# Token-major copies of layer 1 made by VectorE block transposition and DMAs through DRAM instead of TensorE transposes

## The chip, the cores and the metric

The kernel runs on one core of a Trainium2 chip. The metric is device time in microseconds (us) from the start to the end of one execution. Three executions of the kernel before gave 2556.81, 2556.70 and 2556.46 us, a median of 2556.7 us.

## The reference, cut to what matters

Two layers over x of shape (4, 128, 64, 64): 4 batches, 128 channels, 4096 positions ("tokens"). Layer 0 is full self-attention over positions behind a group normalization. Layer 1 is causal self-attention and a recurrent feed-forward part, each behind a layer normalization over the 128 channels of a token:

```python
x = x + conv_attention(groupnorm(x))            # layer 0, full attention, queries and keys of 64 channels
t = to_tokens(x)                                # (b, 4096, 128)
t = t + causal_attention(ln_t(t), Wq, Wk, Wv)   # layer 1
t = t + ffn(ln_t(t), W, V, gamma, beta)         # batch norm over all tokens, then
#   y[t] = sigmoid(Wx[t] + y[t-1] @ V.T) along the tokens
def ln_t(v): return (v - mean(v, -1)) / sqrt(var(v, -1) + 1e-5)
```

The kernel holds x channel-major: channels on the 128 partitions, tokens along the free dimension. The layer normalization of a token reduces over channels, so it needs those values token-major: tokens on partitions, channels along the free dimension.

## The kernel before, in words

All arithmetic is fp32 (layer 0's keys and queries are split into two fp32r parts). The code that runs is `fast_kernel`. `general_kernel` is a fallback in a branch that is not taken here.

**Units.** Attention is cut into units. One unit is a pair of 128-row key blocks against one query tile of 512 columns. Layer 0 has 16 units for each of its 8 query tiles, layer 1 has 2(c+1) units for query tile c because it is causal. The order is batch by batch, layer 0 then layer 1, tile by tile: 128 + 72 units for a batch. `score(i)` puts the scores of unit i into a PSUM pair (L923 and L930, two buffers), ScalarE writes their exponentials to a tile `s` in SBUF (L932 and L936, three buffers), and `product(i - 1)` adds the exponentials to `total` on VectorE (L960, L965) and multiplies them by the values on TensorE (L968).

**Tasks between the units.** All other work is written as Python generators, and each `yield` ends a piece. Between `score(i)` and `product(i - 1)` the function `step()` takes one piece of each task in `ends` (the closing of a query tile, `finish`) and one piece of the first task in `todo`. `whole(key)` runs a task to its end at once. It is called where a unit needs the result. The tasks that matter here:

- `prepare1(b, c)` (key `p1`) is put on the list when query tile c of layer 0 is closed. It makes the normalized token-major values V1 and the reciprocal deviations R1 for 512 tokens.
- `ffn(b, c, ...)` (key `f`) is put on the list when query tile c of layer 1 is closed. It stores the tile to DRAM (`kept`, L751, batches 0 to 2), computes the reciprocal deviations of 512 tokens, and multiplies by the FFN weight.
- `after(b, c)` comes before `query1(b, c)`. It calls `whole` on every `p1` up to c.
- `keys0(b + 1, c)`, eight tasks, prepare the keys of the next batch's layer 0.

Both `prepare1` and `ffn` call `deviations` (L693): four TensorE transposes of 128x128 into a PSUM tile `pt` (L698), then on VectorE `bn_stats` (L702) and `bn_aggr` (L704) for each block and an addition (L570), then a power on GpSimd (L571). `prepare1` writes V1 from `pt` with four `tensor_scalar` (L731). `ffn` needs only the reciprocal deviations, which `spread` (L709) brings back channel-major.

**Buffers and queues.** `misc` tiles (PSUM, two buffers) hold `pt` and other small matmul results. `finish` calls `project`, which lets a stated number of pieces pass and then issues the matmul `po` (L831) and the residual addition (L834). SyncE issues the DMAs of X, of `kept` and of the reload at the end (L508, L751, L1015). After the attention the recurrence runs in chunks (L1045 to L1155). The order on an engine is not always the written order: the build may place an instruction that is ready ahead of one that waits.

Of the kernel before, what the change touches and what calls it, by code (L numbers as in the profile page):

```python
# [25 lines left out]
F32 = mybir.dt.float32  # L26
AF = mybir.ActivationFunctionType
ALU = mybir.AluOpType
# [446 lines left out]
def fast_kernel(  # L475
# [97 lines left out]
    with ExitStack() as actx:  # L573
# [10 lines left out]
        def misc(name):  # L584
            return ps_m.tile([P, QT], F32, tag="m", name=name)
# [104 lines left out]
            Q[b, 0, c] = q  # L690
            yield

        def deviations(src, eps, name):  # L693

            n = src.shape[-1] // P
            pt = misc(f"pt_{name}")
            for j in range(n):
                nc.tensor.transpose(pt[:, ts(j, P)], src[:, ts(j, P)], ident)  # L698
            stats = small.tile([P, 4, 6], F32, tag="lst", name=f"lst_{name}")
            mv = small.tile([P, 4, 2], F32, tag="lmv", name=f"lmv_{name}")  # L700
            for j in range(n):
                nc.vector.bn_stats(stats[:, j, :], pt[:, ts(j, P)])  # L702
            for j in range(n):
                nc.vector.bn_aggr(mv[:, j, :], stats[:, j, :])  # L704
            rstd = small.tile([P, 4], F32, tag="rstd", name=f"rstd_{name}")
            rsqrt(rstd[:, :n], mv[:, :n, 1], eps, n)
            return pt, mv, rstd[:, :n]

        def spread(r, name):  # L709

            n = r.shape[-1]
            g = small.tile([P, 4, 4], F32, tag="g", name=f"g_{name}")
            for q in range(4):
                nc.vector.tensor_copy(g[0:32, :n, q], r[ds(32 * q, 32), :])
            for q in range(1, 4):
                nc.vector.tensor_copy(g[ds(32 * q, 32), :n, :], g[0:32, :n, :])
            rb = tmp.tile([P, QT], F32, tag="r", name=f"rb_{name}", bufs=2)[:, : n * P]
            nc.vector.transpose(
                rb.rearrange("p (k j) -> p k j", j=32),
                g[:, :n, :].rearrange("p j q -> p (j q)").unsqueeze(2).to_broadcast([P, 4 * n, 32]),  # L720
            )
            return rb

        def prepare1(b, c):
            if c == 0:
                V1[b] = kv.tile([P, NB, C], F32, tag="V1", name=f"V1_{b}")
                R1[b] = small.tile([P, NB], F32, tag="R1", name=f"R1_{b}")
            pt, mv, rstd = deviations(X[b][:, ts(c, QT)], 1e-5, f"1_{b}_{c}")
            nc.gpsimd.tensor_copy(R1[b][:, ts(c, 4)], rstd)
            for j in range(4):  # L730
                nc.vector.tensor_scalar(  # L731
                    V1[b][:, 4 * c + j, :], pt[:, ts(j, P)], mv[:, j, 0:1], rstd[:, j : j + 1],
                    ALU.subtract, ALU.mult,
                )
            yield

# [9 lines left out]
        def ffn(b, c, off, w):  # L746
            name = f"f_{b}_{c}_{off}"
            cols = ds(c * QT + off, w)
            src = X2[b][:, cols]
            if b < len(kept):  # L750
                nc.sync.dma_start(out=kept[b][:, cols], in_=src)  # L751
            yield
            _, _, rstd = deviations(src, 1e-5, name)
            yield
            pw = misc(f"pw_{name}")[:, :w]
            if off == 0:
                wt[b, c] = tmp.tile([P, QT], F32, tag="w", name=f"w_{name}")
            part = wt[b, c][:, ds(off, w)]
            if w == QT - LAST:
                nc.tensor.matmul(pw, lhsT=FWc, rhs=src, start=True, stop=True)  # L760
                raw = tmp.tile([P, QT], F32, tag="a", name=f"raw_{name}")[:, :w]
                nc.scalar.copy(raw, pw)
                prow = misc(f"prow_{name}")
                idle(prow, 7)
                nc.tensor.matmul(prow[:, :w], lhsT=rstd.to_broadcast([P, P]), rhs=ident, start=True, stop=True)
                nc.vector.tensor_tensor(part, raw, prow[:, :w], ALU.mult)
                idle(misc(f"idle_{name}"), 5)
            else:
                rb = spread(rstd, name)
                nc.tensor.matmul(pw, lhsT=FWc, rhs=src, start=True, stop=True)  # L770
                nc.vector.tensor_tensor(part, pw, rb, ALU.mult)
            if w < QT:
                yield
            nc.scalar.copy(
                WX[b][:, :, ds((c * QT + off) // CHUNK[b], w // CHUNK[b]), :].rearrange("p l s t -> p s l t"),
                part.rearrange("p (s l t) -> p s l t", l=CHUNK[b] // 2, t=2),
            )
            if off + w == QT:
                nc.vector.bn_stats(stats_f[:, b * NQ + c, :], wt.pop((b, c)))
            yield  # L780

        def finish(b, layer, c, off, w, av, total):

            name = f"{layer}_{b}_{c}_{off}"
            k = w // 32
            if w == QT - LAST:

                pz = misc(f"pz_{name}")
                for h in range(2):
                    nc.tensor.matmul(pz[:, :w], lhsT=ones, rhs=total[:, h, :w], start=h == 0, stop=h == 1)  # L790
                idle(misc(f"idle_{name}"), 4)
                rb = tmp.tile([P, QT], F32, tag="a", name=f"rb_{name}")[:, :w]
                nc.vector.reciprocal(rb, pz[:, :w])
                o = tmp.tile([P, QT], F32, tag="b", name=f"o_{name}")[:, :w]
                nc.vector.scalar_tensor_tensor(o, rb, GUARD, av[:, :w], ALU.mult, ALU.mult)
                yield from project(b, layer, c, off, w, o, 0)
                return
            t = tmp.tile([P, QT], F32, tag="a", name=f"t_{name}")[:, :w]
            nc.vector.tensor_tensor(t, total[:, 0, :w], total[:, 1, :w], ALU.add)  # L799
            tt = tmp.tile([P, QT], F32, tag="b", name=f"tt_{name}")[:, :w]  # L800
            nc.vector.transpose(tt, t)  # L801
            part = small.tile([P, 16], F32, tag="part", name=f"part_{name}")
            nc.vector.tensor_reduce(part[:, :k], tt.rearrange("p (k j) -> p k j", j=32), AX.X, ALU.add)
            yield
            side = small.tile([32, 4, 16], F32, tag="side", name=f"side_{name}")
            for q in range(4):
                nc.vector.tensor_copy(side[:, q, :k], part[ds(32 * q, 32), :k])
            z = small.tile([P, 16], F32, tag="z", name=f"z_{name}")
            nc.vector.tensor_reduce(z[0:32, :k], side[:, :, :k].rearrange("j q k -> j k q"), AX.X, ALU.add)
            nc.vector.reciprocal(z[0:32, :k], z[0:32, :k])  # L810
            for q in range(1, 4):
                nc.vector.tensor_copy(z[ds(32 * q, 32), :k], z[0:32, :k])
            rb = tmp.tile([P, 16, 32], F32, tag="a", name=f"rb_{name}")[:, :k, :]
            nc.vector.transpose(rb, z[:, :k].unsqueeze(2).to_broadcast([P, k, 32]))  # L814
            o = tmp.tile([P, QT], F32, tag="b", name=f"o_{name}")[:, :w]
            nc.vector.scalar_tensor_tensor(  # L816
                o, rb.rearrange("p k j -> p (k j)"), GUARD, av[:, :w], ALU.mult, ALU.mult
            )
            yield from project(b, layer, c, off, w, o, 2 if w == QT else 5)

        def project(b, layer, c, off, w, o, waits):
            cols = ds(c * QT + off, w)
            xt = X[b][:, cols]
            if layer == 0:
                nc.vector.scalar_tensor_tensor(xt, o, 1.0 / GUARD, xt, ALU.mult, ALU.add)
                yield
                return
            for _ in range(waits):
                yield
            po = misc(f"po_{b}_{c}_{off}")[:, :w]  # L830
            nc.tensor.matmul(po, lhsT=W1v, rhs=o, start=True, stop=True)  # L831
            if c == 0:
                X2[b] = xpool.tile([P, N], F32, tag="X2", name=f"X2_{b}")
            nc.vector.scalar_tensor_tensor(X2[b][:, cols], po, 1.0 / GUARD, xt, ALU.mult, ALU.add)  # L834
            yield
# [4 lines left out]
        for b in range(B):  # L840
            for layer in range(2):
                for c in range(NQ):
                    parts = [(0, LAST), (LAST, QT - LAST)] if (b, layer, c) == (B - 1, 1, NQ - 1) else [(0, QT)]
                    for off, w in parts:
                        n = (c * QT + off + w) // P if layer else NB
                        units += [(b, layer, c, off, w, u, n) for u in range((n + 1) // 2)]
        todo, ends, made = [], [], {}

        def put(key, g):
            made[key] = g  # L850
# [132 lines left out]

        def step():

            for key in list(ends) + todo[:1]:
                if (key in ends or key in todo) and next(made[key], "done") == "done":
                    done(key)

        for _ in gn_stats(0):  # L990
            pass
# [204 lines left out]
```

## Time and profile before

| what | value |
|---|---|
| median of three runs | 2556.7 us |
| profiled execution | 2556.64 us |
| its span, first to last instruction | 2554.8 us |
| VectorE busy | 1771.1 us (69%), 3534 instructions |
| ScalarE busy | 1139.8 us (45%) |
| GpSimd busy | 194.7 us (8%) |
| DMA, mean over the span | 12 GB/s |
| mean granted TensorE clock | 0.997 |

The profile is of one execution. "Busy" is the time in which at least one instruction of an engine runs. Matmuls are pipelined, so TensorE's busy time says little about what one instruction costs. For that the reader wants the distance between the starts of neighbours, or the chain of work that ended last, which gives each piece the time for which it held up the end.

### The profile page before, as it was taken

Reading aid. Unit: us, or ns where it says so; the run is one execution under the profiler, and the core shown is the slowest. Engines: PE = TensorE matmul, PEld = TensorE weight load, DVE = VectorE, ACT = ScalarE, POOL = GpSimd, SP = SyncE. Lnnn points to the kernel's source line nnn. Section 1 sums busy time; section 2 is a strip of 40 time slices with the busy share of each in tenths; the row PEclk is TensorE's granted clock in tenths of the full one; section 3 lists DMA queues with packets and bytes.
Section 4 is the critical chain, followed back from the end, with each engine's and each line's share of the span. In section 5 each row is a group of like instructions: output and inputs, shape, how many; then the busy total and the mean of one; then the engine's idle time right before and its main releaser. Section 6 shows DMA issues by size and latency. Waiting matters only on the chain.

```text
span 2554.8 us, 22329 instructions
## 1 busy us (share of the span) xinstructions
PE 2506.5 (98%) x7612; PEld 1367.5 (54%) x7612; DVE 1771.1 (69%) x3534; ACT 1139.8 (45%) x1432; POOL 194.7 (8%) x281
## 2 busy tenths in 40 slices
PE   7999999999999999999999999999999999999997
PEld 4555554444555555444455555444455555544465
DVE  6776667656867667656777676855677675786567
ACT  4444444444444444444444444444444444444456
POOL 2010001101000100110000010011010000010000
PEclk9999999999999999999999999999999999999999
DMA  2000000000100000000100000000010000000013
GB/s 73 1 0 1 0 1 13 9 5 4 38 0 1 1 0 5 13 4 5 33 9 0 1 0 1 9 9 8 5 38 0 1 1 1 1 1 0 0 66 133
DMA packets 11946, 31.33 MB, mean 12 GB/s; under 512 B 2096, under 2 KB 2864, under 8 KB 10032
## 3 DMA queue, kind: packets, MB, share of 16 engines
q1 hardware_dynamic: 9216, 26.22, 2.8%
q10 hardware_dynamic: 2608, 3.61, 0.4%
q8 instruction: 61, 1.00, 0.2%
q14 instruction: 61, 0.50, 0.1%
HBM read 15.14 MB, written 14.68 MB: 12 GB/s over the span
## 4 chain that ended last, share of the span: by engine, by line
PE 88%; DVE 7%; ACT 2%; issue 1%; POOL 1%; POOLq 0%; DVEq 0%; ACTq 0%
PE av L968 48%; PE ps L930 17%; PE ps L923 16%; DVE total L965 2%; PE pv L675 1%; PE po L831 1%; PE pk L659 1%; PE pq L740 1%; PE pw_f L770 1%; PE pt L698 1%; ACT WX L1061 1%; ACT s L932 0%; POOL rstd_f L571 0%; PE pt_f L698 0%; PE pz L1060 0%
## 5 line engine op out<-in xcount | busy, mean ns | idle before, releaser
L965 DVE TENSOR_TENSOR total<-total,s 128x1024 f32<-128x1024 f32 (+5 forms) x810 | 882.1, 1092 | 561.0 <-ACT s L932 323.0
L968 PE MATMUL av<-s,WXp 128*128 128x512 f32 x2048 | 963.9, 593 | 1.7 <-ACT s L932 1.7
L932 ACT ACTIVATE s<-ps,shift 128x1024 f32<-128x1024 f32 x512 | 569.6, 1114 | 751.7 <-PE ps L930 728.3
L930 PE MATMUL ps<-q,K 128*128 128x512 f32 x2048 | 758.5, 492 | 1.0 <-DVE K L670 0.9
L936 ACT ACTIVATE s<-ps,zero,R 128x512 f32<-128x512 f32 (+3 forms) x607 | 405.1, 718 | 462.0 <-PE ps L923 460.5
L968 PEld LDWEIGHTS av<-s,WXp 128*128 128x128 f32 x2048 | 381.9, 189 | 299.1 <-issue 256.1
L930 PEld LDWEIGHTS ps<-q,K 128*128 128x128 f32 x2048 | 386.3, 189 | 289.7 <-issue 235.2
L968 PE MATMUL av<-s,V 128*128 128x512 f32 (+3 forms) x1214 | 505.0, 538 | 2.0 <-ACT s L936 1.7
L923 PE MATMUL ps<-q,X 128*128 128x512 f32 (+3 forms) x1214 | 503.5, 537 | 0.0
L923 PEld LDWEIGHTS ps<-q,X 128*128 128x128 f32 x1214 | 224.9, 190 | 236.3 <-issue 219.5
L968 PEld LDWEIGHTS av<-s,V 128*128 128x128 f32 x1214 | 222.0, 190 | 224.5 <-issue 195.6
L571 POOL TENSOR_TENSOR rstd<-rstd,mhalf 128x4 f32<-128x4 f32 x32 | 32.7, 1022 | 964.3 <-DVE rstd L570 964.3
L656 POOL TENSOR_SCALAR X<-X,B0v 128x512 f32<-128x512 f32 x32 | 67.6, 2114 | 250.9 <-DVE xg L654 249.4
L939 POOL TENSOR_SCALAR_AFFINE_SELECT s<-s 128x128 f32<-128x128 f32 x128 | 46.3, 366 | 519.5 <-ACT s L936 519.1
L731 DVE TENSOR_SCALAR V<-pt,lmv,rstd 128x128 f32<-128x128 f32 x128 | 43.7, 404 | 35.7 <-POOL rstd L571 35.7
L571 POOL TENSOR_TENSOR rstd_f<-rstd_f,mhalf 128x4 f32<-128x4 f32 (+2 forms) x33 | 35.8, 1086 | 406.3 <-DVE rstd_f L570 406.3
L689 DVE TENSOR_TENSOR q<-QR,qh 64x512 fp32r<-64x512 f32 x64 | 43.8, 685 | 6.3 <-PE ps L930 5.7
L671 ACT CAST K<-kh 64x512 fp32r<-64x512 f32 x32 | 19.7, 617 | 62.1 <-DVE kh L669 62.1
L799 DVE TENSOR_TENSOR t<-total 128x512 f32<-128x512 f32 x64 | 44.1, 689 | 4.4 <-PE pfw L615 2.5
L801 DVE STREAM_TRANSPOSE tt<-t 128x512 f32<-128x512 f32 x64 | 45.3, 708 | 1.9
L816 DVE SCALAR_TENSOR_TENSOR o<-rb,av 128x512 f32<-128x512 f32 x64 | 43.6, 682 | 4.1
L814 DVE STREAM_TRANSPOSE rb<-z 128x512 f32<-128x512 f32 x64 | 45.0, 703 | 1.1
(156 smaller groups left out, 1311.2 us busy)
## 6 DMA issues: line engine op xcount, KB each, us to landing
X<-in_x SPq DMA_DIRECT2D x28, 256.0 KB, 5.3
kept<-X SPq DMA_DIRECT2D x24, 256.0 KB, 2.0
Y<-kept SPq DMA_DIRECT2D x6, 1024.0 KB, 7.7
out<-Y SPq DMA_DIRECT2D x5, 1024.0 KB, 6.0
X<-in_x ACTq DMA_DIRECT2D x4, 256.0 KB, 5.5
out<-Y ACTq DMA_DIRECT2D x1, 1024.0 KB, 6.7
out<-X SPq DMA_DIRECT2D x1, 1024.0 KB, 10.9
out<-X ACTq DMA_DIRECT2D x1, 1024.0 KB, 13.3
```

The lines of the kernel that those rows point to most:

```text
L571: nc.gpsimd.tensor_tensor(dst, dst, mhalf[:, :n], ALU.pow)
L656: nc.gpsimd.tensor_scalar(xt, xt, B0v, None, ALU.add)
L799: nc.vector.tensor_tensor(t, total[:, 0, :w], total[:, 1, :w], ALU.add)
L801: nc.vector.transpose(tt, t)
L814: nc.vector.transpose(rb, z[:, :k].unsqueeze(2).to_broadcast([P, k, 32]))
L923: nc.tensor.matmul(ps[:, h, first[h] : w], lhsT=lhsT, rhs=q[:, off + first[h] : off + w], start=True, stop=True,)
L930: nc.tensor.matmul(ps[:, h, :], lhsT=lhsT, rhs=q[:, k, :], start=k == 0, stop=k == 1)
L932: nc.scalar.activation(s, ps, AF.Exp, bias=shift)
L936: nc.scalar.activation(part, ps[:, h, first[h] : w], AF.Exp, scale=scale, bias=zero)
L939: nc.gpsimd.affine_select(out=edge, in_=edge, pattern=[[1, P]], base=0, channel_multiplier=-1, compare_op=ALU.is_ge, fill=0.0,)
L965: nc.vector.tensor_tensor(t, t, s[:, h, f:w], ALU.add)
L968: nc.tensor.matmul(av[:, first[h] : w], lhsT=V[:, 2 * u + h, :], rhs=s[:, h, first[h] : w], start=u == 0 and h == 0, stop=2 * u + h == n - 1,)
```

## The change

`deviations` no longer transposes. It takes a token-major view `tok`. A new generator `turn` makes that view: VectorE transposes each 32x32 block of 128x512 (`nc.vector.transpose`), one DMA writes the result to a DRAM tile, and four DMAs, one for each group of 32 partitions, read it back in runs of 32 elements (128 bytes), so that each partition holds one token's channels in each of its four blocks. The destination is V1 itself in `prepare1`, which then normalizes it in place, and the turned tile in `ffn`. `turn` then yields 5. `step()` now skips a task for a stated number of units and takes the first task that does not wait. At most two turns are open at once. A third waits by yielding 1 up to eight times, then runs the oldest to its end. The last tile of the last batch keeps the TensorE transposes. The tile `r` goes from two buffers to one, `t` with two buffers is new, and `project` waits three pieces instead of two for the last tile of a batch.

```diff
-        def deviations(src, eps, name):
-
-            n = src.shape[-1] // P
-            pt = misc(f"pt_{name}")
-            for j in range(n):
-                nc.tensor.transpose(pt[:, ts(j, P)], src[:, ts(j, P)], ident)
+        def deviations(tok, n, eps, name):
+
...
-                nc.vector.bn_stats(stats[:, j, :], pt[:, ts(j, P)])
+                nc.vector.bn_stats(stats[:, j, :], tok[:, j, :])
...
+        turning = []
+
+        def turn(src, dst, name, key):
+
+            for _ in range(8):
+                if len(turning) == 2:
+                    yield 1
+            while len(turning) == 2:
+                whole(turning[0])
+            turning.append(key)
+            t = tmp.tile([P, QT], F32, tag="t", name=f"t_{name}", bufs=2)
+            nc.vector.transpose(t, src)
+            d = dram.tile([P, QT], F32, tag="turn", name=f"turn_{name}", bufs=4)
+            nc.sync.dma_start(out=d, in_=t)
+            if dst is None:
+                dst = t.rearrange("p (j c) -> p j c", c=C)
+            view = d.rearrange("(i r) (j q s) -> q r j i s", i=4, q=4, s=32)
+            for q in range(4):
+                nc.sync.dma_start(
+                    out=dst[ds(32 * q, 32)].rearrange("r j (i s) -> r j i s", i=4), in_=view[q]
+                )
+            yield 5
+            turning.remove(key)
+            return dst
...
-            rb = tmp.tile([P, QT], F32, tag="r", name=f"rb_{name}", bufs=2)[:, : n * P]
+            rb = tmp.tile([P, QT], F32, tag="r", name=f"rb_{name}")[:, : n * P]
...
-            pt, mv, rstd = deviations(X[b][:, ts(c, QT)], 1e-5, f"1_{b}_{c}")
+            tok = V1[b][:, 4 * c : 4 * c + 4, :]
+            yield from turn(X[b][:, ts(c, QT)], tok, f"1_{b}_{c}", ("p1", b, c))
+            mv, rstd = deviations(tok, 4, 1e-5, f"1_{b}_{c}")
             nc.gpsimd.tensor_copy(R1[b][:, ts(c, 4)], rstd)
             for j in range(4):
                 nc.vector.tensor_scalar(
-                    V1[b][:, 4 * c + j, :], pt[:, ts(j, P)], mv[:, j, 0:1], rstd[:, j : j + 1],
-                    ALU.subtract, ALU.mult,
+                    tok[:, j, :], tok[:, j, :], mv[:, j, 0:1], rstd[:, j : j + 1], ALU.subtract, ALU.mult,
                 )
...
-            _, _, rstd = deviations(src, 1e-5, name)
+            if (b, c) == (B - 1, NQ - 1):
+                pt = misc(f"pt_{name}")
+                for j in range(w // P):
+                    nc.tensor.transpose(pt[:, ts(j, P)], src[:, ts(j, P)], ident)
+                tok = pt.rearrange("p (j c) -> p j c", c=C)
+            else:
+                tok = yield from turn(src, None, name, ("f", b, c, off))
+            _, rstd = deviations(tok, w // P, 1e-5, name)
...
-            yield from project(b, layer, c, off, w, o, 2 if w == QT else 5)
+            yield from project(b, layer, c, off, w, o, 5 if w < QT else 3 if c == NQ - 1 else 2)
...
+            ready = [key for key in todo if pause.get(key, 0) <= 0][:1]
+            for key in pause:
+                pause[key] -= 1
+            for key in list(ends) + ready:
+                if key in ends or key in todo:
+                    got = next(made[key], "done")
+                    if got == "done":
+                        done(key)
+                    elif got:
+                        pause[key] = got
```

More of the change, by code (lines that the diff above doesn't have):

```diff
@@ L706, in deviations @@
             rsqrt(rstd[:, :n], mv[:, :n, 1], eps, n)
-            return pt, mv, rstd[:, :n]
+            return mv, rstd[:, :n]
+        turning = []
[20 more added lines that the diff above has]
+            return dst
         def spread(r, name):
@@ L846, in fast_kernel @@
                         units += [(b, layer, c, off, w, u, n) for u in range((n + 1) // 2)]
-        todo, ends, made = [], [], {}
+        todo, ends, made, pause = [], [], {}, {}
         def put(key, g):
@@ L984, in step @@
         def step():
-            for key in list(ends) + todo[:1]:
-                if (key in ends or key in todo) and next(made[key], "done") == "done":
-                    done(key)
+            ready = [key for key in todo if pause.get(key, 0) <= 0][:1]
[8 more added lines that the diff above has]
+                        pause[key] = got
         for _ in gn_stats(0):
```

## Prediction

> **What bounds the kernel now.** I read the busy shares first, then the chain of work that ended last in small windows, because a busy share doesn't price an instruction here.
>
> ```profile
> PE 2506.5 (98%) x7612; PEld 1367.5 (54%) x7612; DVE 1771.1 (69%) x3534; ACT 1139.8 (45%) x1432; POOL 194.7 (8%) x281
> PE 88%; DVE 7%; ACT 2%; issue 1%; POOL 1%; POOLq 0%; DVEq 0%; ACTq 0%
> ```
>
> TensorE is busy 98% of the span and holds 88% of the chain. VectorE has 31% to spare on the average. The chain in layer 0 of batch 0 (start us, us on the chain, what) gives the price of the four transposes:
>
> ```profile
> 303.00 0.70 PE ps L930 x3
> 303.70 0.43 PE pt L698 x4
> 304.13 1.72 PE av L968 x4
> 305.86 0.93 PE ps L930 x4
> 306.78 1.72 PE av L968 x4
> ```
>
> TensorE never stops here. A unit of layer 0 is 0.93 + 1.72 = 2.65 us, and one group of four transposes adds 0.43 us (0.44 in layer 1's windows). The by-form groups show why the busy column would mislead:
>
> ```profile
> L698 PE MATMUL pt_f<-ident,X 128*128 128x128 f32 x128 | 19.4, 273 | 0.4 <-DVE X L834 0.4
> L698 PE MATMUL pt<-ident,X 128*128 128x128 f32 x128 | 19.4, 274 | 0.8 <-DVE X L825 0.8
> ```
>
> 273 ns is the latency of one, and 19.4 us for 32 groups is 0.61 us each because it counts the last one's drain, which lies under the next matmul. The true slot is 0.435 us.
>
> VectorE matters where layer 1 ends and the next batch begins. The windows (us, then busy of PE, PEld, DVE, ACT, POOL, granted clock, DMA share, GB/s):
>
> ```profile
> 635.00:655.00 20.00, 17.79 (x63) 10.62 (x62) 16.86 (x53) 9.50 (x12) 3.19 (x5) 1.00 0.00 1
> 655.00:675.00 20.00, 20.00 (x59) 10.85 (x58) 18.39 (x44) 6.37 (x7) 2.01 (x2) 0.91 0.35 118
> 715.00:735.00 20.00, 20.00 (x62) 11.40 (x61) 10.79 (x10) 9.26 (x10) 0.00 (x0) 1.00 0.00 1
> ```
>
> VectorE is at 84 to 92% there against 54% in a quiet stretch, TensorE loses 2.2 us, and the clock drops right after. The timeline names the wait:
>
> ```profile
> 653.16 0.66 DVE L816 SCALAR_TENSOR_TENSOR o<-rb,av 128x512 f32<-128x512 f32 x1
> 653.88 1.12 PE L831 MATMUL po<-o,W1v 128*128 128x512 f32 x2 [2.21 <-DVE o L816]
> ```
>
> The closing of a batch's last tile is late on VectorE, and TensorE, in order, stands before `po`. The same stands at 1267 and 1880 us: three times some 2.4 us.
>
> **What the Trainium skill says.** "TensorE: Matmul & The Clock Gate", Part 4, puts a transpose at about 275 ns in one kernel's context. The trace agrees on the latency (273 ns), but the slot is 435 / 4 = 109 ns, and that decides. "VectorE: DVE Perf Modes", The three transpose paths: VectorE transposes only separate 32x32 blocks, so the blocks must still be moved between partitions, here by DMA. The trace has the instruction at this size (L801, 708 ns). "DMA: Bandwidth & Descriptors", Two DMAs through the same engine are not ordered: a read of what an earlier DMA wrote needs a wait on its semaphore at the issuing engine. No run here shows such a pair yet. I take it that SyncE stands between the write and the four reads.
>
> **The change, part by part**, against the profiled execution of 2556.64 us (span 2554.8), which is the median of 2556.7 for this purpose.
>
> *Transposes.* 32 tiles of `prepare1` and 31 of `ffn` (the last tile keeps its own): 63 groups x 0.435 = **-27.4 us** on the path. `pt` leaves the `misc` buffers too; no wait on it shows, so nothing is taken for that.
>
> *VectorE.* 63 block transposes x 0.71 = +44.7 us. `bn_stats` costs the same from SBUF (281 ns for 128 columns from PSUM; 682 ns for 512 from SBUF, L622: both are columns / 0.96 plus 148). V1's `tensor_scalar` now reads SBUF: L654 (SBUF, 512 columns) takes 562 ns, L664 (PSUM) 740. I put 128 columns at 360 ns against 404, so -6 us for 128; the bounds are 160 and 404. VectorE goes from 1771 to about 1810 us, 71%. In layers' middles this lies beside TensorE and costs 0. At the three batch boundaries, where VectorE is short, six FFN tiles fall into layer 0's small units: 6 x 0.71 = 4.3 us of new work each, 12.8 us in all. The cover is there for most, since the pauses also spread the tiles (two in twelve units, before one in four). I charge a third: **+4.2 us** (0 to 12.8).
>
> *The round trip.* SyncE issues 5 DMAs for each turn. A store of 256 KB lands in 2.0 us and a load of 256 KB in 5.3 us behind others:
>
> ```profile
> X<-in_x SPq DMA_DIRECT2D x28, 256.0 KB, 5.3
> kept<-X SPq DMA_DIRECT2D x24, 256.0 KB, 2.0
> ```
>
> Four reads of 64 KB, 0.33 to 0.5 us to issue each, in 2048 packets of 128 bytes. The trace's packets take 18 ns at 256 bytes and 27 at 512, so I estimate 13.5 ns at 128: 128 for each of 16 engines, 1.7 us. Write 2.0 + issue 0.3 + reads 3.3 to 6.5: **5.6 to 9 us**, doubled at worst if short packets write badly. The pause: `yield 5` is set after that step's count, and counted down before the list is read, so the task returns six steps later: 6 x 2.65 = 15.9 us in layer 0, 6 x 3.44 = 20.6 in layer 1. Hidden, cost 0. Without that cover, VectorE stands at `bn_stats`, and all `total` additions are queued behind it.
>
> *The forced turns.* Walking the task list by hand: `p1(b, 7)` for b = 0, 1, 2 comes behind eight `keys0` tasks, and `after(b, 7)`, at the head when tile 6 begins (unit 42 of layer 1), calls `whole` on it. The pause is passed over, so write, reads and `bn_stats` fall in one step. Three times VectorE may stand 5.6 to 9 us. Behind it are the `total` additions; those free the three `s` buffers, so exponentials and then TensorE wait. Around that place (531 to 548 us) the exponential at 547.9 us needs a `total` that ended at 544.7: 3.2 us of slack. But instructions written later already run ahead there (the closing's four steps, 530.3 to 533.1, precede the `bn_stats` at 533.07), which fills some 2.8 us. 5.6 + 0.7 - 3.2 - 2.8 is about nothing; 9 + 0.7 - 3.2 is 6.5, and a lowered clock adds 1.7 (at 655.5 to 658 matmuls took 0.85 instead of 0.43 us). I take 2 each: **+6.0 us** (0 to 24.6).
>
> *SyncE's queue.* 63 x (5 issues of 0.4 + a stand of 2.0) = 252 us of 2555. Queued behind are `kept` (wanted at the end), the reload of Y (likewise) and X of the next batch. X's eight loads (656.7 to 669 us, at full DMA rate) meet FFN turns twice and delay them by up to 10 us: 9 + 10 against a pause of 15.9. I charge 1 us each: **+2.0 us** (0 to 6). GpSimd's power and copies keep their counts, ScalarE's too.
>
> *`po` waits one unit more* for a batch's last tile: 2.65 us more for VectorE, where 3 x 2.4 us stand now, but VectorE has more to do. I take half: **-3.5 us** (0 to -9, with the clock drop of batch 0). `r` with one buffer: writer and reader are both VectorE, 0. At most two turns at once delays FFN tiles by some units; the FFN recurrence needs them only at the end, and by my walk the last turn of batch 3 returns 19 units ahead of it: 0.
>
> Sum: -27.4 + 4.2 + 6.0 + 2.0 - 3.5 = -18.7, so **2538 us**.
>
> **Rivals.**
> *A, the forecast:* most of TensorE's time is kept. 2530 to 2547; chance 0.50.
> *B, everything is hidden:* forced turns are filled by other work and `po` no longer waits: 2556.7 - 27.4 - 9 = 2520 us. For it: 31% of VectorE is free, and the build orders by readiness. Against: the boundary is at 92% already. Chance 0.20.
> *C, given back:* the forced turns cost their upper bound, 24.6, and the boundary 4.2: 2556.7 - 27.4 + 28.8 = 2558 us; with only part of it, down to 2547. Against: the fill seen at 531 us. Chance 0.18.
> *D, slower:* the round trip outlasts the pause. It would do so at the 46 turns that run in layer 0 (28 of `p1`, about 18 of `ffn`). TensorE feels it past 15.9 + 3.2 = 19.1 us, and it eats the gain past 19.1 + 27.4 / 46 = 19.7 us. At 21 us: 46 x 1.9 = 87, giving 2556.7 - 27.4 + 87 = 2617 us. For it: 2048 short packets for each turn, of which the trace before has no like. Against: the estimate is under half of it. Chance 0.12.
>
> **How the numbers follow.** A difference of 0.2% (5.1 us) is about what a measurement of this kernel can tell from no change. A, B and about 0.08 of C lie under 2551.6: faster 0.78. The rest of C is within: 0.10. D: slower 0.12. The range 2522 to 2556 leaves out D and a little of B and C.
>
> **What would show it.** Right: no `pt` on the chain in the middle of layer 0, units at 2.65 us, `bn_stats` waiting on a DMA only at three places near the middle of layer 1, reads landing under 9 us. Boundary: windows after each batch's end with VectorE at 90% and TensorE losing no more than now. Wrong: VectorE waiting for DMAs at most turns (D), or TensorE losing over 6 us at each forced turn (C). A TensorE slot saved that is not 0.43 us would upset the first term.

## The result, and the profile after

The changed kernel takes **2517.1 us** (median of four executions, 2516.93 to 2517.82) against 2556.6 for the kernel before beside it. The ratio is 0.9843, with a 95% interval of 0.983 to 0.9855: 39.5 us less, where 18.7 were forecast. The time lies below the range. The profiled execution took 2517.08 us, its span is 2515.3.

Busy times and the shares of the chain of work that ended last, of the changed kernel:

```profile
PE 2472.7 (98%) x7360; PEld 1341.6 (53%) x7360; DVE 1797.5 (71%) x3597; ACT 1141.4 (45%) x1432; POOL 210.6 (8%) x281
PE 92%; DVE 4%; ACT 2%; issue 1%; POOL 1%; DVEq 0%; POOLq 0%
```

VectorE does 26 us more, and yet its share of the chain falls from 7% to 4%, and TensorE's rises from 88% to 92%. That hints that waits for VectorE went too. It prices nothing: 3% of the span is 77 us, more than the whole gain. Where `pt` stood in layer 0, the chain now runs on:

```profile
299.82 1.72 PE av L997 x4
301.53 0.93 PE ps L959 x4
302.46 1.72 PE av L997 x4
304.18 0.93 PE ps L959 x4
```

The boundary of batch 0, in windows (us, then busy of PE, PEld, DVE, ACT, POOL, granted clock, DMA share, GB/s):

```profile
627.00:647.00 20.00, 20.00 (x65) 11.63 (x64) 17.19 (x39) 10.73 (x13) 2.20 (x4) 1.00 0.01 2
647.00:667.00 20.00, 20.00 (x62) 11.27 (x60) 17.93 (x37) 8.46 (x8) 0.88 (x1) 1.00 0.51 144
667.00:687.00 20.00, 20.00 (x61) 11.14 (x60) 17.05 (x36) 10.03 (x11) 0.13 (x1) 1.00 0.00 0
```

VectorE is as full as before, 85 to 90%, but TensorE loses nothing and the clock stays at 1.00. The timeline has `po` with no idle time before it, where it had 2.21 us:

```profile
645.24 1.02 PE L860 MATMUL po<-o,W1v 128*128 128x512 f32 x2
```

The new path itself, from the list of DMA issues (count, KB each, median us from issue to landing):

```profile
turn<-t SPq DMA_DIRECT2D x32, 256.0 KB, 2.0
V<-turn SPq DMA_DIRECT2D x128, 64.0 KB, 2.5
turn_f<-t_f SPq DMA_DIRECT2D x31, 256.0 KB, 2.0
t_f<-turn_f SPq DMA_DIRECT2D x124, 64.0 KB, 2.6
```

In the waits, SyncE stands 58.5 us in 32 waits and 55.8 in 31 between write and reads, 1.8 each. The four reads take 2.59 us to issue (at 387.4 us in the timeline). A turn is 0.3 + 1.8 + 2.6 + 2.5, about 7 us. VectorE's only waits for a DMA are these (us in total, times, longest):

```profile
DVE stats L622 <- DMA X<-in_x: 8.5, 4, 4.7
```

They are for X, none for a turn. What I had not foreseen is when things happen. The statistics of the FFN's tiles, before and then after (durations, then first and last start in us):

```profile
L702 DVE BATCH_NORM_STATS2 lst_f<-pt_f x128: 258/281/300, 580.5 to 2476.9; 128x6 f32<-128x128 f32 x128
```

```profile
L698 DVE BATCH_NORM_STATS2 lst_f<-t_f x124: 251/277/295, 419.3 to 2397.9; 128x6 f32<-128x128 f32 x124
```

Before, the first came at 580.5 us, the batch's eight between there and 683. After, they begin at 419.3, 430.3, 454.8, 476.8, 512.7, 556.6, 605.6 and 661.9 us, soon after each tile is closed. The turn of `p1(b, 7)` is issued at 385.3 us, though the code writes it near 530. So the build has placed these instructions where their operands are ready. With the transposes on TensorE this did not happen: in the kernel before, TensorE transposes that tile at 531.3 us, near its written place, and the statistics follow at 533.

**An account of stalls.** From the matmul records between 90 and 2400 us I add up what a start-to-start distance has over the usual slot of its kind, wherever TensorE stood idle in it. Before: 14.5 us. Among them are three `po` of 2.36 to 2.40, nine `av<-s` and `pt` of 0.17 to 0.94, and three `pq` of 1.13. After: 5.4 us, three `pq` of 1.47 and three `av<-s` of 0.32. Matmuls that were too long without any idle time, at half clock, are counted apart. Before they make 1.7 us: behind the first `po` stall, two `pw_f` and four `av` held the chain for 1.58 and 2.69 us instead of 0.86 and 1.72. After there are none. So 27.4 us of slots, 9.1 of stalls and 1.7 of half clock make 38.2 of the 39.5. (The stall sums in the recorded expectations below come from another count and are 1 to 3.4 us higher than those of the text.)

### The profile page after: what moved, and what is told of

Its sections match the earlier page's. It is cut to its first block, busy times and chain, and to the rows that moved or that the text cites. A ratio compares the mean times of both kernels' runs of the same rounds, so it can differ in the third digit from the quotient of the medians.

```text
span 2515.3 us, 22534 instructions
## 1 busy us (share of the span) xinstructions
PE 2472.7 (98%) x7360; PEld 1341.6 (53%) x7360; DVE 1797.5 (71%) x3597; ACT 1141.4 (45%) x1432; POOL 210.6 (8%) x281
## 3 DMA queue, kind: packets, MB, share of 16 engines
q1 hardware_dynamic: 151344, 59.27, 8.9%
## 4 chain that ended last, share of the span: by engine, by line
PE 92%; DVE 4%; ACT 2%; issue 1%; POOL 1%; DVEq 0%; POOLq 0%
PE av L997 51%; PE ps L959 19%; PE ps L952 17%; PE pw_f L799 1%; PE pv L675 1%; PE pq L762 1%; PE po L860 1%; DVE total L994 1%; PE pk L659 1%; ACT WX L1097 1%; PE pz L1096 0%; ACT first L1097 0%; ACT WXp L1097 0%; POOL X L656 0%; ACT s L961 0%
## 5 line engine op out<-in xcount | busy, mean ns | idle before, releaser
L968 POOL TENSOR_SCALAR_AFFINE_SELECT s<-s 128x128 f32<-128x128 f32 x128 | 52.5, 416 | 458.1 <-ACT s L965 454.2
L571 POOL TENSOR_TENSOR rstd_f<-rstd_f,mhalf 128x4 f32<-128x4 f32 (+2 forms) x33 | 47.4, 1435 | 507.9 <-DVE rstd_f L570 507.9
L754 DVE TENSOR_SCALAR V<-V,lmv,rstd 128x128 f32<-128x128 f32 x128 | 38.0, 342 | 33.6 <-POOL rstd L571 33.5
```

Source lines behind the costliest of these rows:

```text
L571: nc.gpsimd.tensor_tensor(dst, dst, mhalf[:, :n], ALU.pow)
L968: nc.gpsimd.affine_select(out=edge, in_=edge, pattern=[[1, P]], base=0, channel_multiplier=-1, compare_op=ALU.is_ge, fill=0.0,)
```

## The experiments

Theory: 27.4 us are slots, and the other 12 are boundary stalls that went because the statistics no longer hang on TensorE's order. Rivals for the 12: `po`'s third waited piece, or the pause, which spreads the tiles.

**The third waited piece alone, and its removal.** First it is undone in the changed kernel, as shown here; then it is made, without the rest, in the kernel before.

```diff
-            yield from project(b, layer, c, off, w, o, 5 if w < QT else 3 if c == NQ - 1 else 2)
+            yield from project(b, layer, c, off, w, o, 5 if w < QT else 2)
```

> The changed kernel with the third waited piece of project taken back (2 for a batch's last tile, as before). Theory po-wait (the three 2.4 us stalls before po went because po is issued one unit later): the stalls return, 2517 + 7 to 11 = 2524 to 2528 us. Theory early work (the FFN statistics no longer queue behind TensorE's transposes and run early in layer 1, so VectorE is no longer short at the batch boundary): 2517 to 2519 us.

> The kernel before with only project's third waited piece added. Theory po-wait: the stalls before po go, 2556.6 - 7 to 11 = 2546 to 2550 us. Theory early work: VectorE stays short at the boundary and the stall only shifts, 2553 to 2557 us.

Measured: 2517.51 us (2517.01 to 2518.92), no different from the changed kernel; and 2560.17 (2556.3 to 2562.19), ratio 1.001 (1.0002 to 1.0019). The wait brings nothing. Alone it takes the three `po` stalls away, but the stalls rise to 17.6 us and the half clock behind them to 4.7: TensorE now stands before `av` at 673, 1290 and 1904 us (3.67, 3.66, 1.89 us).

**The pause away:**

```diff
-            yield 5
+            yield
```

> The changed kernel with yield 5 replaced by a plain yield, so a turned task is taken up again one unit later. Theory pause (the five units hide the round trip): VectorE stands about 6.8 us - 2.65 us at each of some 60 turns, of which 3.2 us is slack, so 2517 + 60 x 1 = about 2570 us or more. Theory early work (the build places the statistics where the data is ready, whatever the written order): 2517 to 2522 us.

Measured: 2517.49 us (2516.94 to 2518.26), stalls 5.4. The pause hides nothing that the placement doesn't hide already.

**Each group of transposes twice,** in the kernel before:

```diff
-            for j in range(n):
-                nc.tensor.transpose(pt[:, ts(j, P)], src[:, ts(j, P)], ident)
+            for _ in range(2):
+                for j in range(n):
+                    nc.tensor.transpose(pt[:, ts(j, P)], src[:, ts(j, P)], ident)
```

> The kernel before with every group of transposes issued twice into the same tile. It measures the slot: at 0.435 us for a group of four, 64 groups (two smaller ones make up the last) add 27.8 us, 2584 us. If TensorE's transposes cost more than their slot (by the wait of VectorE's statistics behind them), more than that, up to 2595 us.

Measured: 2584.78 us (2583.26 to 2587.95), 27.9 more, where 64 slots of 0.435 us are 27.8. Its executions lie 4.7 us apart, so the sum is good to some 2 us; within that the slot stands.

**Two more copies in DRAM for each turn,** ahead of the reads:

```diff
+            for k in range(2):
+                e = dram.tile([P, QT], F32, tag=f"hop{k}", name=f"hop{k}_{name}", bufs=4)
+                nc.sync.dma_start(out=e, in_=d)
+                d = e
```

> The changed kernel with two more DMAs from DRAM to DRAM in each turn, so that the round trip grows from about 6.8 us by some 4 to 6 us. If the round trip is hidden because the build places the statistics where the data has landed: 2516 to 2519 us. If it is hidden by little (the slack of three score buffers): 63 turns x 1 to 3 us, 2570 us and more.

Measured: 2519.98 us (2519.39 to 2520.18), 2.9 more than the changed kernel. The stalls grow by 2.9: VectorE waits for a turn in four places (1.5 us at most), and the three stands before an `av`, 0.3 us in the changed kernel, are 1.3 us, at 414, 1018 and 1621 us. The two copies take 2.9 us each to land, so a trip grows from about 7 to some 13 us, and nearly all of that is still hidden. The 19 us from which rival D expects a loss were not reached.

**Each half alone.** In the first, `ffn` keeps its TensorE transposes; in the second, `prepare1` does:

```diff
-            if (b, c) == (B - 1, NQ - 1):
+            if True:
                 pt = misc(f"pt_{name}")
```

```diff
-            yield from turn(X[b][:, ts(c, QT)], tok, f"1_{b}_{c}", ("p1", b, c))
-            mv, rstd = deviations(tok, 4, 1e-5, f"1_{b}_{c}")
+            pt = misc(f"pt_1_{b}_{c}")
+            for j in range(4):
+                nc.tensor.transpose(pt[:, ts(j, P)], X[b][:, ts(c * 4 + j, P)], ident)
+            pt = pt.rearrange("p (j c) -> p j c", c=C)
+            mv, rstd = deviations(pt, 4, 1e-5, f"1_{b}_{c}")
...
-                    tok[:, j, :], tok[:, j, :], mv[:, j, 0:1], rstd[:, j : j + 1], ALU.subtract, ALU.mult,
+                    tok[:, j, :], pt[:, j, :], mv[:, j, 0:1], rstd[:, j : j + 1], ALU.subtract, ALU.mult,
```

> The changed kernel, but every ffn tile keeps its TensorE transposes; only prepare1's 32 tiles are turned. Theory early work (the FFN statistics set the boundary stalls): the slot of 32 x 0.435 = 13.9 us and little more, 2541 to 2544 us. Theory of an even share (each tile's turn brings the same): half of 39.8, 2537 us.

> The changed kernel, but prepare1's 32 tiles keep their TensorE transposes; only 31 ffn tiles are turned. Theory early work: 31 x 0.435 = 13.5 us and the 11 us of the boundaries, 2530 to 2533 us. Theory of an even share: 2537 us.

Measured: 2545.45 us (2544.78 to 2547.5), 11.9 less than before; 2544.53 (2543.25 to 2546.71), 12.8 less. Both are about their own slots (13.9 and 13.5). Together the halves give 24.7, the whole gives 39.5. Stalls are 17.0 and 15.6 us, no fewer than the 14.5 of before. At first sight the theory that early FFN statistics clear the boundary falls here, for the second kernel turns the FFN. But its FFN statistics are not early:

```profile
L698 DVE BATCH_NORM_STATS2 lst_f<-t_f x124: 245/278/296, 535.0 to 2425.3; 128x6 f32<-128x128 f32 x124
```

The block transpositions of the first two tiles run at 411.5 and 418.4 us, much as in the changed kernel. Their statistics begin at 535.0, right behind those of `prepare1` for tile 7, whose TensorE transposes run at 531.2 and statistics at 533.0, as before. The third tile is transposed only at 552.5, and the last two statistics of batch 0 come at 706.2 and 715.4, inside the next batch. With only `prepare1` turned, the FFN's come at 576.0 to 680.8 us, about as before. So neither half has early FFN statistics, and neither tests that theory. It takes both turns to get them. What holds the FFN's statistics behind those of `prepare1` was not tested.

**The tie given back without the transposes.** A product of one column and a copy of one number stand ahead of each FFN turn's block transposition, so that it must wait for its place in TensorE's order:

```diff
+            if dst is None:
+                gate = misc(f"gate_{name}")
+                nc.tensor.matmul(gate[0:1, 0:1], lhsT=src[:, 0:1], rhs=ident[:, 0:1], start=True, stop=True)
+                nc.vector.tensor_copy(t[0:1, 0:1], gate[0:1, 0:1])
```

> The changed kernel with one more TensorE matmul of one column in each of the 31 ffn turns, whose result VectorE copies into the tile ahead of the block transposition, so that the ffn turns wait for their written place in TensorE's order again, with the transposes themselves still gone. Theory early work: the 11 us at the boundaries come back, and the matmuls cost 31 x 0.1 to 0.25 = 3 to 8 us: 2530 to 2537 us. If only the slot of the transposes counted: 2520 to 2525 us.

Measured: 2541.74 us (2541.32 to 2546.62), 24.6 over the changed kernel. The FFN's statistics are late again, from 587.9 us on instead of 419.3, the last of batch 0 at 717.4. Stalls are 16.3 us, 10.9 more, half clock adds 3.3, and the 31 products take some 0.2 us each of TensorE. Those are 21 of the 24.6; where the last 3 to 4 lie I did not find. The position in TensorE's order is what costs; the transposes' own time is not needed for it. (The product also takes a `misc` buffer, which a turn does not. No run separates the two.)

**How a late VectorE reaches TensorE.** The chain of the kernel before with only the third piece, at its largest stall:

```profile
660.80 0.45 PE pt_f L698 x4
661.25 0.28 SPq L508
661.53 0.05 issue
661.58 4.61 DMA X<-in_x
666.19 0.02 issue
666.22 0.69 DVE stats L622
...
674.68 0.68 DVE w_f L771
675.36 0.02 issue
675.38 0.02 ACT WX L774
...
675.93 1.11 ACT s L932
677.04 0.04 issue
677.08 3.78 PE av L968 x4
```

Read it downwards. The load of X needs a buffer that the transposes of an FFN tile were the last to read. VectorE stands at `bn_stats` for it and is then late with `w_f`. ScalarE stands at the copy into WX for `w_f`, the exponentials are queued behind that copy, and TensorE waits for the exponential. ScalarE's side, in the timeline of the kernel with only `prepare1` turned:

```profile
671.57 0.65 ACT L803 COPY WX<-w_f 128x512 f32<-128x512 f32 x1 [6.08 <-DVE w_f L800]
672.11 2.11 ACT L961 ACTIVATE s<-ps,shift 128x1024 f32<-128x1024 f32 x2
```

and its TensorE:

```profile
673.27 1.22 PE L997 MATMUL av<-s,WXp 128*128 128x512 f32 x1 [3.65 <-ACT s L961]
```

The Trainium skill, "PSUM — Partial Sum Buffer", Engine vs sequencer instructions, says that ScalarE's, VectorE's and GpSimd's queues are strict FIFO and that matmuls start in program order. The trace agrees: the scores of the next exponentials had ended by 669.6 us, and both came right behind the copy, at 672.11. ScalarE's longest stand for `w_f` sorts the kernels: 3.7 us in the changed kernel, no `av` stall at a boundary; 4.3 before, up to 0.94; 5.3 with only `ffn` turned, 2.2; 5.9 and 6.1 in the two just shown, 3.7 and 3.8. The kernel with the tie given back is out of line: 6.2, but only 2.0. What makes VectorE late is not always the same. With only `ffn` turned, the eight `bn_stats` of X (656.1 to 668.8 us) are long past; there it is the two late FFN tiles, whose `w_f` come at 716.4 and 724.9 us.

**That door shut.** If this is the way, the lateness must lose its effect when the copy goes to GpSimd (8% busy):

```diff
-            nc.scalar.copy(
+            (nc.gpsimd.tensor_copy if w == QT else nc.scalar.copy)(
                 WX[b][:, :, ds((c * QT + off) // CHUNK[b], w // CHUNK[b]), :].rearrange("p l s t -> p s l t"),
```

> The FFN's transposes on TensorE, the layer-1 preparation by the new path (2545.45 us by itself, 18.2 us of stalls, 13.8 of them av<-s at the three boundaries), with the copy into WX on GpSimd. Theory (lateness handed on through ScalarE's order): those 13.8 us go, 2531 to 2535. Rival (s buffers held by late sums): 2543 to 2547.

> The kernel before with the third waited piece for po (2560.2 us by itself, with 21.0 us of TensorE stalls in layer 0 and 1) and, beside it, the FFN's copy into WX moved from ScalarE to GpSimd. Theory (VectorE, held up by bn_stats waiting for an X chunk whose buffer TensorE's late transposes had held, gives its lateness on through ScalarE: the copy into WX waits for w_f and the exponentials stand behind it): the av<-s stalls at each boundary (about 5 us, three times, with the 0.4 to 0.9 after them) go, and the time falls by 12 to 17 us to 2543 to 2548. Rival (VectorE's late sums hold the three s buffers, whichever engine copies): the stalls stay, 2557 to 2562.

> The layer-1 preparation's transposes on TensorE, the FFN by the new path (2544.53 us by itself, 16.6 us of stalls), with the copy into WX on GpSimd. Theory (lateness handed on through ScalarE's order behind w_f): the av<-s stalls of 2.23, 2.23 and 2.27 us early in each layer 0, and the 0.98 after the last, go; those of 0.91 us in layer 1, which end in the chain QR, kh, K and not in WX, and the waits ahead of pq stay: 2536 to 2538. Rival (the transposes of the preparation hold TensorE themselves): 2543 to 2546.

Measured: 2530.35 us (2530.2 to 2531.81), 15.1 less than without the edit, stalls 4.9; 2557.92 (2556.72 to 2560.51), 2.2 less, stalls 13.9 and half clock 3.4; 2540.81 (2540.05 to 2542.11), 3.7 less, stalls 14.0. The first came out as the theory had it, slightly better. The other two missed its number, and the second lies where its rival put it. And yet their boundary `av` stalls, too, are gone, which that rival would have kept. Others stand in their place. The timeline of TensorE in the second:

```profile
701.70 1.11 PE L698 MATMUL pt<-ident,X 128*128 128x128 f32 x4 [4.20 <-DVE X L825]
```

and in the third:

```profile
740.14 0.66 PE L752 MATMUL pt<-ident,X 128*128 128x128 f32 x4 [1.54 <-DVE X L857]
```

That is the second door. `pt` is `prepare1`'s own transpose of the first tile that layer 0 of the next batch closes; it needs the residual addition into X, VectorE gives that late, and TensorE, in order, stands. Only kernels that keep `prepare1` on TensorE have this door. With it gone and the copy moved, no boundary stall over 0.5 us is left, though the FFN is still transposed on TensorE.

**The largest stalls left.** The three `pq` of 1.47 us come right behind VectorE's bias addition into QR. It is moved to ScalarE:

```diff
-            nc.vector.tensor_scalar(
-                QR[b][ds(half * CQ, CQ), ts(col, QT)], pk[low, :], B0qk[low, :], None, ALU.add
-            )
+            nc.scalar.activation(
+                QR[b][ds(half * CQ, CQ), ts(col, QT)], pk[low, :], AF.Identity, bias=B0qk[low, :]
+            )
```

> The changed kernel with the bias addition into QR (0.75 us of VectorE) on ScalarE. The three stalls of 1.47 us ahead of pq, each right behind that addition, are the only ones left. Theory that this addition sets them: 3 to 4.4 us less, 2512.7 to 2514. Rival (VectorE is late by more than that one instruction): 2516 to 2518.

Measured: 2520.59 us (2519.61 to 2521.55), 3.5 more; both theories missed. The `pq` stalls are gone. They were not the only ones left, as I had it: the three stands of 0.3 us before an `av` are now 2.2 us, at 413, 1018 and 1621 us, with 3.3 us of half clock behind them. The chain there:

```profile
413.00 2.47 POOL X L656
415.46 0.26 POOL s L968
415.72 0.04 issue
415.77 2.49 PE av L997 x3
```

GpSimd's addition into X stands ahead of the causal mask of an exponential. Relief on one engine ended at a wait in another's queue. No version beat the changed kernel.

## Why the prediction was wrong

It was wrong by 21 us, all to one side: four terms in which VectorE and the queues gave back or won little.

*Transposes, -27.4:* right. Doubling them added 27.9.

*VectorE, and what is hidden:* right. VectorE 1797.5 us against about 1810. V1 from SBUF takes 342 ns against the 360 I took:

```profile
L754 DVE TENSOR_SCALAR V<-V,lmv,rstd 128x128 f32<-128x128 f32 x128 | 38.0, 342 | 33.6 <-POOL rstd L571 33.5
```

*The round trip, 5.6 to 9 us:* about 7. But "the pause: 15.9 us" was not what hid it. Without the pause the time is the same.

*The forced turns, +6.0 (0 to 24.6):* this step failed. I walked the written list and put write, reads and `bn_stats` of `p1(b, 7)` into one step near 530 us. In the trace its turn is issued at 385 us and its statistics begin at 397. No wait came. I had noted that the build runs ready instructions ahead and used it for 2.8 us of fill, not for the place of the whole turn. The 3.2 us of slack were misread as well. The exponential at 547.9 us came so late because ScalarE stood in front of it, at a cast that waited for VectorE, the door that the experiments found later:

```profile
547.26 0.62 ACT L671 CAST K<-kh 64x512 fp32r<-64x512 f32 x1 [3.05 <-DVE kh L669]
547.90 1.45 ACT L936 ACTIVATE s<-ps,zero,R 128x512 f32<-128x512 f32 x2
```

*The boundary, +4.2, and X's loads, +2.0:* failed in the same way. Both assumed six FFN turns at the boundary; of batch 0's eight, six had begun their statistics by 557 us. What I added to the boundary had left it.

*`po`, -3.5:* the right place, the wrong cause and size. The term of the sum is the stalls that go, and it measured -9.1, of which `po`'s own are 7.2, with -1.7 of clock. The third piece gave none of it. It came because both ties to TensorE's order were cut: the FFN's own, and `prepare1`'s, behind which the FFN's statistics also stand and through which VectorE's lateness reaches TensorE directly. In the changed kernel the eight `bn_stats` of X lie between two tiles of the FFN instead of inside one. They start at 652.4 to 665.9 us and the next `w_f` at 671.8, before which VectorE waits for TensorE:

```profile
665.88 0.68 DVE L622 BATCH_NORM_STATS2 stats<-X 128x6 f32<-128x512 f32 x1
...
671.81 0.69 DVE L800 TENSOR_TENSOR w_f<-pw_f,rb_f 128x512 f32<-128x512 f32 x1 [1.13 <-PE pw_f L799]
```

With only `prepare1` turned they start at 661.8 to 675.5 us, and a `w_f` at 670.9 stands in their midst. This order alone does not clear the boundary: with only `ffn` turned, and with the tie given back, they lie between two tiles as well (656.1 to 668.8 and 660.2 to 670.2 us), and TensorE stands all the same.

Of the rivals, B ("everything is hidden", 2520 us) was nearest. I held the full boundary against it, and that was the error: 85 to 90% busy is harmless once nothing late is in the way of ScalarE's or TensorE's next step. C and D found nothing to act on.

The stall account against the medians (each against the kernel before beside it):

| kernel | slots | stalls | half clock | their sum | measured |
|---|---|---|---|---|---|
| changed | -27.4 | -9.1 | -1.7 | -38.2 | -39.5 |
| only `prepare1` turned | -13.9 | +2.6 | -0.1 | -11.4 | -11.9 |
| only `ffn` turned | -13.5 | +1.1 | 0 | -12.4 | -12.8 |
| only `prepare1`, copy on GpSimd | -13.9 | -9.6 | -1.7 | -25.2 | -27.0 |
| only `ffn`, copy on GpSimd | -13.5 | -0.5 | -1.7 | -15.7 | -16.5 |
| third piece alone | 0 | +3.1 | +3.0 | +6.1 | +3.3 |

(Of the last, the traced execution was the slowest of twelve, 2562.19 us.)

Shown are the slot, the two doors, that a place in TensorE's order brings stalls back without the transposes, and that neither the third piece nor the pause matters. That the FFN's early statistics are what frees the boundary in the changed kernel is read from the traces: they are early there, and late in both halves and with the tie given back. No run moved them alone. Late ones did no harm where both doors were shut. Open are the 0.4 to 2.8 us by which the sums miss, and what holds the FFN's statistics back when only `ffn` is turned.

## What to carry to other kernels

Work that hangs on a full in-order engine happens when its turn comes, which can be long after its data is ready. Taking it off that engine frees the time it took and also moves all that follows to another time, so look for the waits at its old place, and price a new one from where the build puts the instructions, not from the written order. When an engine is late, ask in which queue the next engine stands for it, and what is queued behind that one instruction.

## What the runs showed of the hardware

A read of 64 KB in 512 runs of 128 bytes took 0.56 to 0.69 us to issue on SyncE in all but 2 of 252 cases, against 0.33 for the write of 256 KB in front of it. It landed in 2.5 us, the write in 2.0. The queue of these DMAs went from 9216 packets to 151344 and from 2.8% to 8.9% of the engines' time, and X's loads landed in 5.1 us instead of 5.3.

The clock dropped after a stand shorter than I would have looked for. The windows of the kernel before behind the first two `po` stalls (columns as above):

```profile
654.00:659.00 5.00, 5.00 (x9) 2.10 (x9) 4.32 (x15) 0.00 (x0) 1.01 (x1) 0.66 0.35 112
1267.00:1272.00 5.00, 4.26 (x12) 2.22 (x13) 4.33 (x16) 0.00 (x0) 1.01 (x1) 1.00 0.19 68
```

The Trainium skill, "TensorE: Matmul & The Clock Gate", Part 1, gives half rate after at least one idle window of some 3.4 us. Here a stand of 2.21 us was followed by matmuls at 0.85 us, half rate, in batch 0, and one of the same length was not in batch 1. Nor does the length alone sort the cases. With only `prepare1` turned, a stand of 3.65 us was followed by a granted clock of 0.69 over 5 us, and one of 3.29 us by 1.00; with the tie given back, one of 1.87 us was followed by 0.66. On the length the measurement decides, and what else decides is open. A stall of this size can cost 1.7 us more than itself.
